# A fused attention and feed-forward kernel: the side work of an attention turn, and how many blocks of weighted sums go into the same turn

## The chip, the core and the metric

The kernel runs on one core of a Trainium2 chip. The metric is device time in microseconds (us) of one execution. The engines that matter are PE (TensorE matmuls), PEld (its weight loads), ACT (ScalarE, which computes the exponentials), DVE (VectorE), POOL (GpSimd) and the DMA queues.

## What is computed

Four sequences of 1024 tokens with 256 features go through attention with 16 heads of 16 features, and then through a gated feed-forward net with ternary weights. Layer norms surround both, and all of it is float32.

```python
qkv = layernorm(x) @ Wqkv.T                              # (4, 1024, 3*256)
scores = einsum('bhqd,bhkd->bhqk', q, k) / sqrt(16)      # 16 heads, 1024 x 1024 each
e = exp(clip(scores - max, -50, 50))
attn = e / (e.sum(-1) + 1e-6)
x = x + layernorm((attn @ v) @ Wout.T)
h = silu(ln(x) @ w1 * s1) * (ln(x) @ w2 * s2)            # 256 -> 1024
h = gelu(h @ h1 * s3); h = gelu(h @ h2 * s4)             # 1024 -> 1024, twice
x = x + layernorm(h @ w3 * s5)                           # 1024 -> 256
```

## The kernel before

The attention takes the first half of the time and is written as one long loop over **tiles** (L444). A tile is one sequence b, one group g of four heads, one half h of the queries (512 of them), one run c of 128 keys and one pair u of heads. There are 4 x 4 x 2 x 8 x 2 = 512 tiles. `exponentials(k)` (L450) makes one tile: two matmuls of 64 rows give the scores `s` in one of three PSUM buffers of two banks (L172), and one ACT instruction writes their exponentials `e` into a ring of eight tiles (RING, L27). `weigh(k)` (L460) takes two tiles, which are the four heads of one run of keys, and adds one **block** of weighted sums to `acc`: four products, which the profile counts as eight matmuls. Eight blocks make a **unit** (b, g, h). `rise(k)` (L467) lets DVE keep a running maximum `top` of those exponentials.

One pass of the loop at L874 is a **turn**. It makes three tiles (TURN, L28), weighs the blocks of all tiles that were made before this turn, and ends with `side.take()` (L569). With three tiles a turn and two a block, turns with one block and turns with two blocks alternate. A turn in which a unit ends stops at the end of the unit.

`Side` holds chains of steps. `take` runs down the chains and runs every step that is due: its gap, counted in turns since the step before it in its chain, has passed. Of the steps marked `tensor`, which use PE, it runs at most one in a turn. These tensor steps are:

- the projections of queries and keys (`project`, L325, 16 matmuls `p` in the profile), of values (`values`, L315, `pv`) and of the attention's output (`ending.project`, L517, `py`);
- four transposes of 128x128 (`pt` L310, `po` L512, `fpt` L692);
- the division of a finished unit (L476: eight transposes `po`, L484 and L486), which also borrows one of the three score buffers, so that the next turn makes its third tile only after its blocks (`side.borrowed`);
- sums of squares (`bound`, L360, `pn`) and one final gauge (`flag`, L378, `pr`), which together check that the exponentials can't overflow. For them ACT squares the rounded queries and keys (`squares`, L340).

All of them but the division write to the one bank of `ps_misc` (L174), from which DVE copies the result.

The steps of the next sequence are made by `prologue(b + 1)` while the present one is computed: norms and transposes to `xT`, the projections `qk[0]` of the first eight heads, from the end of group 1 on the values `v` and, five turns later, the projections `qk[1]` of the other eight heads, and then the checks. At the end of a unit `stack` (L425) sends the DMAs that lay out queries and keys for the group after the next, and `slots` (L431) lets POOL copy its values. Asserts hold that what they read has been projected by then. Chains of `check_weights` (L237) round the feed-forward weights in the same turns, on POOL and DVE.

After the last turn the feed-forward net runs (L809), for eight halves of sequences in turn. It is not touched by the change.

Of the kernel before, what the change touches and what calls it, by code (L numbers as in the profile page):

```python
# [70 lines left out]
class Step:  # L71


    def __init__(self, run, gap=0, tensor=True):
        self.run, self.gap, self.tensor = run, gap, tensor
# [39 lines left out]
def tile_fast(ctx: ExitStack, tc: tile.TileContext, x, wqk, wv, wo, w1, w1s, w2, w2s, h1, h1s, h2, h2s, w3, w3s, out, bad):  # L115
# [61 lines left out]
    with ExitStack() as actx, ExitStack() as rctx:  # L177
# [98 lines left out]
        def prologue(b, space, copy):  # L276
# [6 lines left out]
            def gather(h, i):  # L283
                def run():
                    if h == i == 0:
                        st["xT"] = work.tile([P, DC, S], F32, tag="xT", name=f"xT_{b}", bufs=1)
                    st["mv", h] = norms.gather(rows(h)[i : i + 2], i, st.get(("mv", h)))

                return run
# [16 lines left out]
            def transposes(h, c):  # L306
                def run():
                    pt = space(f"pt_{b}_{h}_{c}")
                    for i in range(TPQ):
                        nc.tensor.transpose(pt[:, i * P : (i + 1) * P], st["xn"][:, i, c * P : (c + 1) * P], ident)  # L310
                    copy(st["xT"][:, c, h * NQ : (h + 1) * NQ], pt)

                return run
# [24 lines left out]
            kinds = [(w, m) for w in range(2) for m in range(DC)]  # L338

# [8 lines left out]
            def total(m):  # L348
                def run():
                    if m == 0:  # L350
                        st["norm"] = work.tile([P, NT], F32, tag="norm", name=f"norm_{b}", bufs=1)
                        st["sum"] = work.tile([P, DC], F32, tag="sum", name="sum", bufs=1)
                        st["sum2"] = work.tile([P, DC], BF16, tag="sum2", name="sum2", bufs=1)
# [6 lines left out]
            def bound(h):  # L360


                def run():
                    pn = space(f"pn_{b}_{h}")
                    for k, (w, m) in enumerate(kinds):
                        nc.tensor.matmul(pn[SLOT * k : SLOT * (k + 1), :], heads_bf, st["sq", w, m], start=True, stop=True)
                    nc.vector.tensor_reduce(st["norm"][:, TPQ * h : TPQ * (h + 1)], pn.rearrange("p (t n) -> p t n", n=P), AX.X, ALU.max)
# [10 lines left out]
            def flag():  # L378
# [7 lines left out]
                qs, ks = (pr[0:1, 0 : 2 * P].rearrange("p (i w n) -> p i w n", i=2, w=2)[:, :, w, :] for w in range(2))  # L386
                top = work.tile([1, P // 2], F32, tag="ktop", name="ktop", bufs=1)
                nc.vector.tensor_reduce(top, ks.rearrange("p i n -> p n i"), AX.X, ALU.max)
# [3 lines left out]
                nc.vector.tensor_mul(bounds, qs, top.unsqueeze(1).to_broadcast([1, 2, P // 2]))  # L392
# [10 lines left out]
            qk = [[[Step(project(w, m, h), 1) for w in (1, 0)] for h in range(NH)] for m in range(DC)]  # L403
            v = [Step(values(t), 1) for t in range(0, NT, 2)]
            flags = [Step(total(m), 1, False) for m in range(DC)]
            for h in range(NH):
                flags += [Step(squares(w, m, h), 1, False) for w, m in kinds] + [Step(bound(h), 1)]
            return norm, xt, qk, v, flags + [Step(gauge, 0, False), Step(flag, 1)]
# [92 lines left out]
        def ending(b, h, copy):  # L501
# [41 lines left out]
            def residual(i):  # L543
# [7 lines left out]
                [Step(transposes(c), 1) for c in range(DC)] + [Step(project(t), 1) for t in range(0, TPQ, 2)]  # L551
# [5 lines left out]
        class Side:  # L557


            def __init__(self):  # L560
                self.first, self.rest, self.slot = [], [], 0
                self.borrowed = False
# [5 lines left out]

            def take(self):  # L569
# [3 lines left out]
                free = True  # L573
                for chain in self.first + self.rest:
                    steps = chain[0]
                    while steps and self.slot - chain[1] >= steps[0].gap and (free or not steps[0].tensor):
                        step = steps.pop(0)
                        chain[1] = self.slot
                        step.run()
                        free = free and not step.tensor  # L580

# [5 lines left out]
        accs, tops, ends, later = {}, {}, {}, {}  # L587

        def begin(b):

            if b + 1 < B:
                norm, xt, qk, v, flags = prologue(b + 1, misc, to_vector)

                qk1 = sum(qk[1], [])
                qk1[0].gap = 3
                later["rest"] = v, qk1 + [Step(lambda: side.add(flags), 0, False)]

                later["chain"] = side.add([Step(lambda: None, 0 if b else 4, False)] + sum((norm[h] + xt[h] for h in range(NH)), []) + sum(qk[0], []))

        def unit_end(b, g, h):  # L600
# [6 lines left out]
            if g == NG - 1:  # L607
                unit[0].extend(ending(b, h, to_scalar if (b, h) == (B - 1, NH - 1) else to_vector))
# [9 lines left out]
            if at < B:  # L618
                if at > b:
                    assert not later["chain"][0]  # L620
                stack(at, n)
                slots(at, n)()
            if g == NG - 3 and b + 1 < B:
                v, qk1 = later["rest"]
                assert not later["chain"][0]
                later["chain"][0].extend(v)
                side.add([Step(lambda: None, 5, False)] + qk1)
# [233 lines left out]
        side.add(early + v[2:] + [Step(slots(0, 0), 0, False), Step(slots(0, 1), 0, False)] + sum(qk[1], []) + [Step(lambda: side.add(flags), 0, False)])  # L861
# [4 lines left out]
        def make(end):  # L866

            nonlocal made
            for k in range(made, min(end, len(tiles))):
                assert k - weighed < RING  # L870
# [3 lines left out]
        while weighed < len(tiles):  # L874
            n = made
            make(n + TURN - side.borrowed)
            if made == len(tiles):
                n = made
            for k in range(seen, n - 1, 2):
                rise(k)  # L880
                seen += 2
            while weighed + 2 <= n:
# [9 lines left out]
            make(n + TURN)  # L892
# [243 lines left out]
```

## Time and profile before

| | us |
|---|---|
| three runs | 1326.97, 1328.48, 1330.16; median 1328.48 |
| the profiled execution's own time | 1328.08 |
| its span, from the first to the last instruction | 1326.3 |
| granted TensorE clock, mean | 0.993 |
| PE busy over the span | 1264.8 |
| ACT busy | 697.0 |
| DVE busy | 723.2 |
| POOL busy | 120.5 |

The page lists the costliest groups of instructions with their line, operation, output and input, count, busy time, mean duration, the idle time of the engine just before them and what ended it. These rows are of ACT's exponentials, of the blocks, of the scores and of the gelus of the feed-forward net:

```
L458 ACT ACTIVATE e<-s 128x1024 f32<-128x1024 f32 x512 | 486.3, 1035 | 121.7 <-PE s L457 109.0
L465 PE MATMUL acc<-e,vaug 128*32 128x512 f32 x2048 | 255.1, 600 | 1.4 <-POOL vaug L435 1.4
L457 PE MATMUL s<-sq,sk 64*128 64x512 f32 x1024 | 194.0, 449 | 25.5 <-ACT e L458 22.6
L739 ACT ACTIVATE a<-ph,h_scale 128x512 f32<-128x512 f32 x128 | 81.1, 686 | 306.9 <-PE ph L703 306.9
```

Busy time is the union of a group's instructions: the four matmuls of a block stand side by side in four column strips of the array, so that 2048 matmuls of 600 ns fill 255.1 us. Attention's first score product starts at 27.64 us and its last blocks at 647.37 us; the turns are numbered here from the first pass of the loop, 171 in all. The timeline of an engine lists merged instructions in order: start, duration, line, operation, count, and in brackets how long the engine sat idle before and for whom.

### The profile page before, as it was taken

The numbers are of one execution on the slowest core, as the hardware profiler recorded it, in microseconds if no ns is written. First come the engines' busy times: TensorE is split into PE (matmuls) and PEld (weight loads), VectorE is DVE, ScalarE is ACT, GpSimd is POOL, SyncE is SP. The second block draws the span as 40 slices with busy tenths as digits, with TensorE's granted clock in tenths as the row PEclk, the third lists the DMA queues.
The fourth block names the chain that finished last, engine by engine and source line by source line (L and its number), as shares of the span: only waits on it lengthen the run. The fifth ranks groups of instructions, "written<-read, shape, count | busy, mean of one in ns | idle before, by whom it ended". The sixth has DMA issues, their size and how long they took to land.

```text
span 1326.3 us, 21103 instructions
## 1 busy us (share of the span) xinstructions
PE 1264.8 (95%) x8194; PEld 777.2 (59%) x8194; DVE 723.2 (55%) x1561; ACT 697.0 (53%) x847; POOL 120.5 (9%) x166
## 2 busy tenths in 40 slices
PE   7889999999999999889999999999999999999996
PEld 3333333333333333333478888888888888888885
DVE  3575669756696556646573543636436263362523
ACT  3687788877887787988641422414123141231410
POOL 5221112101121000000010000000000000000000
PEclk8999999999999999999999999999999999999998
DMA  4665444444444333334230000000000000000000
GB/s 127 156 184 128 102 97 116 118 112 121 105 110 110 68 64 65 59 63 166 81 112 0 1 16 1 17 0 6 11 0 17 0 17 0 0 17 0 17 0 20
DMA packets 38670, 79.76 MB, mean 60 GB/s; under 512 B 11296, under 2 KB 21152, under 8 KB 38560
## 3 DMA queue, kind: packets, MB, share of 16 engines
q1 hardware_dynamic: 30672, 53.66, 18.4%
q0 software_dynamic: 7360, 24.12, 5.6%
q8 instruction: 67, 1.10, 0.4%
q10 hardware_dynamic: 528, 0.52, 0.1%
q14 instruction: 43, 0.35, 0.1%
HBM read 28.98 MB, written 15.73 MB: 34 GB/s over the span
## 4 chain that ended last, share of the span: by engine, by line
PE 75%; DVE 12%; ACT 8%; issue 2%; DMA 1%; SPq 1%; ACTq 0%; POOL 0%; POOLq 0%; DVEq 0%
PE ph L703 35%; PE acc L465 12%; PE s L457 8%; ACT e L458 7%; PE pz L756 4%; PE p L268 4%; PE pg L703 4%; PE py L268 2%; DVE top L474 2%; PE pv L268 2%; DVE sg L719 2%; PE po L486 1%; DVE ha_lo L708 1%; DVE o L274 1%; DVE st L93 1%
## 5 line engine op out<-in xcount | busy, mean ns | idle before, releaser
L458 ACT ACTIVATE e<-s 128x1024 f32<-128x1024 f32 x512 | 486.3, 1035 | 121.7 <-PE s L457 109.0
L465 PE MATMUL acc<-e,vaug 128*32 128x512 f32 x2048 | 255.1, 600 | 1.4 <-POOL vaug L435 1.4
L739 ACT ACTIVATE a<-ph,h_scale 128x512 f32<-128x512 f32 x128 | 81.1, 686 | 306.9 <-PE ph L703 306.9
L457 PE MATMUL s<-sq,sk 64*128 64x512 f32 x1024 | 194.0, 449 | 25.5 <-ACT e L458 22.6
L703 PE MATMUL ph<-hb_lo,h 128*128 128x512 f32 x512 | 199.4, 389 | 0.0
L703 PE MATMUL ph<-hb_hi,h 128*128 128x512 f32 x512 | 199.4, 389 | 0.0
L457 PEld LDWEIGHTS s<-sq,sk 64*128 64x128 f32 x1024 | 86.6, 184 | 164.7 <-ACT e L458 126.9
L474 DVE TENSOR_TENSOR top<-top,e 128x512 f32<-128x512 f32 x192 | 133.6, 696 | 35.7 <-ACT e L458 30.2
L740 DVE CAST ha_hi<-a 128x512 fp32r<-128x512 f32 x64 | 27.1, 423 | 157.9 <-ACT a L739 157.9
L465 PEld LDWEIGHTS acc<-e,vaug 128*32 128x32 f32 x2048 | 49.2, 108 | 106.1 <-issue 97.3
L103 POOL TENSOR_TENSOR rstd<-ve,minus_half 128x4 f32<-128x4 f32 (+1 forms) x33 | 37.5, 1137 | 791.1 <-DVE ve L101 791.1
L703 PEld LDWEIGHTS ph<-hb_lo,h 128*128 128x128 f32 x512 | 96.1, 188 | 20.1
L703 PEld LDWEIGHTS ph<-hb_hi,h 128*128 128x128 f32 x512 | 96.1, 188 | 20.2
L703 PE MATMUL ph<-ha_hi,sq 128*128 128x512 f32 x256 | 101.9, 398 | 0.4
L703 PE MATMUL ph<-ha_lo,sq 128*128 128x512 f32 x256 | 99.9, 390 | 0.0
L703 PE MATMUL ph<-ha_lo,sk 128*128 128x512 f32 x256 | 99.8, 390 | 0.0
L703 PE MATMUL ph<-ha_hi,sk 128*128 128x512 f32 x256 | 99.7, 390 | 0.0
L719 DVE SCALAR_TENSOR_TENSOR sg<-pg,w_scale,sg 128x512 f32<-128x512 f32 x64 | 47.1, 745 | 48.4 <-ACT sg L717 48.4
L717 ACT ACTIVATE sg<-pg,w_scale 128x512 f32<-128x512 f32 x64 | 43.4, 689 | 57.2 <-DVE ha_lo L708 48.4
L740 DVE CAST hb_hi<-a 128x512 fp32r<-128x512 f32 x64 | 27.0, 422 | 82.3 <-ACT a L739 82.3
L268 PE MATMUL p<-xT,wqk_sb 128*32 128x512 f32 x512 | 62.3, 608 | 0.9 <-ACT xT L271 0.9
L703 PEld LDWEIGHTS ph<-ha_hi,sq 128*128 128x128 f32 x256 | 48.2, 188 | 12.7 <-DVE sg L719 3.4
(145 smaller groups left out, 1642.9 us busy)
## 6 DMA issues: line engine op xcount, KB each, us to landing
w<-in_h_dram POOLq DMA_DIRECT2D x16, 512.0 KB, 4.5
h_r<-wr POOLq DMA_DIRECT2D x16, 512.0 KB, 3.8
sk<-ck1hi SPq DMA_DIRECT2D x64, 64.0 KB, 2.3
sk<-ck1lo SPq DMA_DIRECT2D x64, 64.0 KB, 2.3
sq<-cq1hi SPq DMA_DIRECT2D x64, 64.0 KB, 2.3
sq<-cq1lo SPq DMA_DIRECT2D x64, 64.0 KB, 2.3
h<-h_r SPq DMA_DIRECT2D x8, 512.0 KB, 7.1
sk<-ck0hi SPq DMA_DIRECT2D x56, 64.0 KB, 2.3
```

Of the source, the lines that this page charges most:

```text
L103: nc.gpsimd.tensor_tensor(rstd[:, :n], ve[:, :n], self.minus_half[:, :n], ALU.pow)
L268: nc.tensor.matmul(o[j : j + SLOT, :], w[:, j : j + SLOT], i, **flags)
L457: nc.tensor.matmul(s[:, a, :], stacks[1, g % 2, u][r, c * P : (c + 1) * P], stacks[0, g % 2, u][r, h * NQ : (h + 1) * NQ], start=True, sto ...
L458: nc.scalar.activation(pair(k)[:, u], s, AF.Exp)
L465: nc.tensor.matmul(acc[SLOT * i : SLOT * (i + 1), :], vaug[g % 2][:, c, i, :], pair(k)[:, i // 2, i % 2, :], start=c == 0, stop=c == NT - 1)
L474: nc.vector.tensor_max(top, top if c > 1 else pair(k - 2)[:, :, :, 0:P], pair(k)[:, :, :, 0:P])
L703: nc.tensor.matmul(p, homes[n][c][:, m * P : (m + 1) * P], half[:, c, :], start=c == 0 and k == 0, stop=c == len(homes[n]) - 1 and k == 1)
L717: nc.scalar.activation(sg, p[:, 0, :], AF.Silu, scale=scales["w1"][:, m : m + 1])
L719: nc.vector.scalar_tensor_tensor(sg, p[:, 1, :], scales["w2"][:, m : m + 1], sg, ALU.mult, ALU.mult)
L739: nc.scalar.activation(a, p[:, j, :], AF.Gelu, scale=scales[n][:, m : m + 1])
L740: nc.vector.tensor_copy(o[0][:, m, :], a)
L756: nc.tensor.matmul(p[t], half[:, c, t * P : (t + 1) * P], homes["w3"][c], start=c == 0 and k == 0, stop=c == HC - 1 and k == 1)
```

## The change

Four things are edited.

**1. A turn's blocks.** Steps get a mark `heavy`: all projections of queries, keys and output, and those of values for b > 0. Before it weighs, the loop asks `side.next_is_heavy()` whether the tensor step that this turn will run is heavy. If so, if two blocks or more are ready, if the ring has room for one tile more in the next turn, and if the next block is not the last but one of its unit, the turn weighs one block only, and the other is left to the turn after it.

**2. Heavy steps not in a row.** A heavy step is also `patient`: it is not due in a turn after one that ran a heavy step (`tired`). Exempt are the steps of `ending`, whose second projection gets a gap of two turns, and `qk[1]` of the sequences after the first, whose steps get a gap of two.

**3. Order of the side work.** The chain of the next sequence makes both halves' statistics first, and puts the normalisation of the second half between the projections of the first. Its first transpose waits until the sequence before has its `qk[1]` and `v` (`ready`), and `xT` is allocated there. `qk[1]` and `v` are appended to the same chain, and `slots` for a next sequence stands in that chain behind `v`.

**4. Sums by eight heads.** `bound(h)` with its four matmuls in one step becomes `bound(m, h)` with two, for m = 0 after `qk[0]` and for m = 1 after `qk[1]`: four steps instead of two for a sequence, each with a DVE maximum over 64 partitions instead of 128. `flag` reads the sums in the new order.

```diff
 class Step:
-    def __init__(self, run, gap=0, tensor=True):
-        self.run, self.gap, self.tensor = run, gap, tensor
+    def __init__(self, run, gap=0, tensor=True, heavy=False):
+        self.run, self.gap, self.tensor, self.heavy = run, gap, tensor, heavy
+        self.ready, self.patient = lambda: True, heavy
...
-            def bound(h):
+            def bound(m, h):
                 def run():
-                    pn = space(f"pn_{b}_{h}")
-                    for k, (w, m) in enumerate(kinds):
-                        nc.tensor.matmul(pn[SLOT * k : SLOT * (k + 1), :], heads_bf, st["sq", w, m], start=True, stop=True)
-                    nc.vector.tensor_reduce(st["norm"][:, TPQ * h : TPQ * (h + 1)], pn.rearrange("p (t n) -> p t n", n=P), AX.X, ALU.max)
+                    pn = space(f"pn_{b}_{m}_{h}")
+                    for w in range(2):
+                        nc.tensor.matmul(pn[SLOT * (2 * m + w) : SLOT * (2 * m + w + 1), :], heads_bf, st["sq", w, m], start=True, stop=True)
+                    own = slice(2 * SLOT * m, 2 * SLOT * (m + 1))
+                    nc.vector.tensor_reduce(st["norm"][own, TPQ * h : TPQ * (h + 1)], pn[own, :].rearrange("p (t n) -> p t n", n=P), AX.X, ALU.max)
...
-            qk = [[[Step(project(w, m, h), 1) for w in (1, 0)] for h in range(NH)] for m in range(DC)]
-            v = [Step(values(t), 1) for t in range(0, NT, 2)]
-            flags = [Step(total(m), 1, False) for m in range(DC)]
-            for h in range(NH):
-                flags += [Step(squares(w, m, h), 1, False) for w, m in kinds] + [Step(bound(h), 1)]
-            return norm, xt, qk, v, flags + [Step(gauge, 0, False), Step(flag, 1)]
+            qk = [[[Step(project(w, m, h), 1, heavy=True) for w in (1, 0)] for h in range(NH)] for m in range(DC)]
+            v = [Step(values(t), 1, heavy=b > 0) for t in range(0, NT, 2)]
+            flags = []
+            for m in range(DC):
+                flags.append([Step(total(m), 1, False)])
+                for h in range(NH):
+                    flags[m] += [Step(squares(w, m, h), 1, False) for w in range(2)] + [Step(bound(m, h), 1)]
+            flags[-1] += [Step(gauge, 0, False), Step(flag, 1)]
+            return norm, xt, qk, v, flags
...
-                [Step(transposes(c), 1) for c in range(DC)] + [Step(project(t), 1) for t in range(0, TPQ, 2)]
+                [Step(transposes(c), 1) for c in range(DC)] + [Step(project(t), 2 if t else 1, heavy=True) for t in range(0, TPQ, 2)]
...
+            def due(self, chain, slot, free):
+                step = chain[0][0] if chain[0] else None
+                if not step or slot - chain[1] < step.gap or step.tensor and not free:
+                    return None
+                return step if step.ready() and not (step.patient and self.tired) else None
+
+            def next_is_heavy(self):
+                for steps, at in self.first + self.rest:
+                    steps = list(steps)
+                    while step := self.due((steps, at), self.slot + 1, True):
+                        if step.tensor:
+                            return step.heavy
+                        at = self.slot + 1
+                        steps.pop(0)
+                return False
...
-                free = True
+                free, heavy = True, False
                 for chain in self.first + self.rest:
-                    steps = chain[0]
-                    while steps and self.slot - chain[1] >= steps[0].gap and (free or not steps[0].tensor):
-                        step = steps.pop(0)
+                    while step := self.due(chain, self.slot, free):
+                        chain[0].pop(0)
                         chain[1] = self.slot
                         step.run()
                         free = free and not step.tensor
+                        heavy = heavy or step.heavy
+                self.tired = heavy
...
+                steps = norm[0] + norm[1] + xt[0]
+                for i, step in enumerate(qk[0][0]):
+                    steps += [step, xt[1][i]]
+                steps += xt[1][TPQ // 2 :] + qk[0][1]
+
+                xt[0][TPQ // 2].ready = lambda: later["qk1"] == later["v"] == b
+                v = v + [Step(lambda: later.update(v=b + 1), 0, False)]
                 qk1 = sum(qk[1], [])
-                qk1[0].gap = 3
-                later["rest"] = v, qk1 + [Step(lambda: side.add(flags), 0, False)]
-
-                later["chain"] = side.add([Step(lambda: None, 0 if b else 4, False)] + sum((norm[h] + xt[h] for h in range(NH)), []) + sum(qk[0], []))
+                for step in qk1:
+                    step.gap, step.patient = 2, False
+                qk1 = qk1 + [Step(second_made, 0, False)]
+                later["rest"] = [Step(lambda: side.add([Step(lambda: None, 5, False)] + qk1), 0, False)] + v
+
+                later["chain"] = side.add([Step(lambda: None, 0 if b else 4, False)] + steps + [Step(first_made, 0, False)])
...
         while weighed < len(tiles):
-            n = made
-            make(n + TURN - side.borrowed)
+            n = end = made
+            end += TURN
+            make(end - side.borrowed)
             if made == len(tiles):
                 n = made
             for k in range(seen, n - 1, 2):
                 rise(k)
                 seen += 2
+
+            if n - weighed >= 4 and made - weighed + TURN - 2 <= RING and tiles[weighed][3] != NT - 2 and side.next_is_heavy():
+                n = weighed + 2
             while weighed + 2 <= n:
...
-            make(n + TURN)
+            make(end)
             if weighed < len(tiles):
                 side.take()
```

`first_made` and `second_made` add the checks of their eight heads as chains and note that the projections are there.

## The prediction

> **What bounds the kernel now.** I first read the busy times by stretch. The columns are the stretch, its length, then busy time and count of PE, PEld, DVE, ACT and POOL, then clock and DMA.
>
> ```profile
> 27.00:646.70 619.70, 579.41 (x4804) 217.87 (x4804) 391.55 (x837) 498.54 (x543) 87.48 (x119) 1.00 0.46 105
> 646.70:1326.30 679.60, 664.78 (x3274) 551.40 (x3270) 320.34 (x687) 191.03 (x292) 19.50 (x18) 0.99 0.05 16
> ```
>
> Only the first stretch, attention, is touched. There PE is busy 93% and ACT 80%. Then the waits of ACT and of PE in the turns (42 to 647 us), in total, times and longest:
>
> ```profile
> ACT e L458 <- PE s L457: 103.7, 110, 2.5
> ...
> ACT e L458 <- DVE top L474: 4.4, 6, 0.8
> ```
>
> ```profile
> PE s L457 <- ACT e L458: 22.6, 62, 0.7
> PE po L484 <- DVE top L474: 6.3, 9, 2.2
> ```
>
> Each of the two waits for the other: some turns are PE's, others ACT's. PE's timeline shows which. First four turns with a projection of the next sequence in each:
>
> ```profile
> 258.26 0.98 PE L457 MATMUL s<-sq,sk 64*128 64x512 f32 x6
> 259.17 1.07 PE L465 MATMUL acc<-e,vaug 128*32 128x512 f32 x8
> 260.05 1.90 PE L268 MATMUL p<-xT,wqk_sb 128*32 128x512 f32 x16
> 261.88 0.96 PE L457 MATMUL s<-sq,sk 64*128 64x512 f32 x6
> 262.77 1.92 PE L465 MATMUL acc<-e,vaug 128*32 128x512 f32 x16
> 264.51 1.90 PE L268 MATMUL p<-xT,wqk_sb 128*32 128x512 f32 x16
> 266.35 0.96 PE L457 MATMUL s<-sq,sk 64*128 64x512 f32 x6
> ```
>
> No bracket, so PE never waits: a turn with a projection and one block takes 261.88 - 258.26 = 3.62 us, with two blocks 266.35 - 261.88 = 4.47. Then turns without a tensor step:
>
> ```profile
> 572.51 0.97 PE L457 MATMUL s<-sq,sk 64*128 64x512 f32 x6
> 573.40 1.07 PE L465 MATMUL acc<-e,vaug 128*32 128x512 f32 x8
> 574.81 0.51 PE L457 MATMUL s<-sq,sk 64*128 64x512 f32 x2 [0.34 <-ACT e L458]
> 575.73 0.50 PE L457 MATMUL s<-sq,sk 64*128 64x512 f32 x2 [0.41 <-ACT e L458]
> 576.64 0.49 PE L457 MATMUL s<-sq,sk 64*128 64x512 f32 x2 [0.42 <-ACT e L458]
> 577.07 1.92 PE L465 MATMUL acc<-e,vaug 128*32 128x512 f32 x16
> 578.92 1.14 PE L457 MATMUL s<-sq,sk 64*128 64x512 f32 x6
> ```
>
> Here PE trickles its scores behind ACT. ACT's own timeline shows its pace and its squares:
>
> ```profile
> 291.30 5.61 ACT L458 ACTIVATE e<-s 128x1024 f32<-128x1024 f32 x6 [1.62 <-PE s L457]
> ...
> 324.55 0.65 ACT L344 ACTIVATE sq<-cq0hi 128x512 bf16<-128x512 f32 x1
> 325.07 2.88 ACT L458 ACTIVATE e<-s 128x1024 f32<-128x1024 f32 x3
> ```
>
> Six exponentials span 5.61, the first 1.03, so one follows another after 0.92 and three need 2.75. A square puts off what follows by 325.07 - 324.55 = 0.52. The pair of turns at 572.51 takes 6.41; two other such pairs (559.45 to 565.25, 623.77 to 629.60) take 5.80 and 5.83; mean 3.0 a turn.
>
> So a turn lasts **the longer of PE's content and about 3.0 us** (2.75 plus handing over), since three score buffers hold one turn's tiles and a long turn saves nothing for the next. PE's content, by pitches without a wait: 1.89 with one block (290.70 to 292.59), 2.75 with two (226.99 to 229.74), 0.86 for one more. A projection adds 1.72 (3.61 - 1.89), and 0.33 more right behind a division (253.46 to 258.26 took 4.80 against 4.47: the scores are split). A division adds 1.47 (250.10 to 253.46 took 3.36), four transposes 0.59, a sum 0.33 (`pn` 142.97 to 143.30), the gauge 0.57.
>
> **The sum before.** I applied the rules of the loop turn by turn, 171 turns in both kernels, for the turns 4 to 170. Before, they run from 41.97 to 646.70: 604.7 us. Counts by blocks in the turn:
>
> | turn holds | before 1 / 2 / 3 | after 1 / 2 / 3 |
> |---|---|---|
> | a projection | 24 / 29 / 0 | 48 / 4 / 1 |
> | a division | 21 / 10 / 0 | 18 / 13 / 0 |
> | another tensor step | 17 / 23 / 0 | 12 / 33 / 3 |
> | none | 22 / 21 / 0 | 11 / 23 / 1 |
>
> Before: projections 24 x 3.61 + 29 x 4.47 + 9 behind a division x 0.33 = 219.2. Divisions 21 x 3.36 + 10 x 4.22 = 112.8. Other steps 17 at the floor of 3.0 and 23 of 3.3 on average (17 transposes 3.34, four sums 3.08, two gauges 3.32) = 126.7. None: 43 x 3.0 = 129.0. Squares fall on turns at the floor and add 10.2 of their 32 x 0.52. Sum 597.9, 1.1% under the 604.7; the rest is about PE's waits for DVE.
>
> **A rule of the Trainium skill** (Perfetto Trace Analysis, Identifying the Most-Contended Engine) says that matmul occupancy is a poor measure of headroom, and that the share of time in LDWEIGHTS and the FLOPs done against the peak are better ones. That share is 217.87 / 619.70 = 35%, by which turns with projections would have room to shrink: if all 53 fell to the floor, 219.2 - 159 = 60 us would go. The four turns at 258.26, which have no gap, speak against it, and no term here rests on the rule.
>
> **Edits 1 and 2.** For example after the end of the second sequence's third unit the turns become: projection and one block, sum and two blocks, projection and one, gauge and two. The rule defers a block in 27 turns. Projections then cost 48 x 3.61 + 4 x 4.47 + 5.33 + 12 x 0.33 = 200.5, **18.7 less**. The blocks land elsewhere: divisions 18 x 3.36 + 13 x 4.22 = 115.3, **2.5 more**. Turns without a tensor step go from 43 to 35 and one block more fits under the floor at no cost: 34 x 3.0 + 3.61 = 105.6, **23.4 less**. That is cover, and where it is gone a block costs 0.86. All 512 tiles still need 171 turns.
>
> **Edits 3 and 4.** Eight sums more (0.33 of content each, and a floor that had hidden nothing else) and the blocks put beside small steps: 48 turns instead of 40, 12 x 3.0, 33 of about 3.25, 3 of 3.9 = 155.1, **28.4 more**. The moved checks put 13 of the 32 squares into turns with a projection, where ACT idles (3.27 against 3.61): squares add 3.8, **6.4 less**. DVE gets eight maxima of 0.69 (the `norm` rows now: 0.684 over 128 partitions; over 64 no row shows it, between 0.34 and 0.69; I take 0.69) and three tiny operations a sequence; it is busy 63%, behind them in its queue are maxima that nobody waits for until a unit ends. `slots` on POOL waits behind `v`: POOL idles for most of the stage and the copy (0.62) is due ten turns later. `stack` is issued at the same unit ends with the same 32 DMAs (267.11 to 290.61 at the end of this unit: 23.5 us, against 11 turns until it is read). The `ready` wait holds only side steps; the asserts' deadlines are met with the last `qk[1]` two turns ahead or more.
>
> The sum: -18.7 + 2.5 - 23.4 + 28.4 - 6.4 = **-17.6**. With a floor of 2.75 instead of 3.0 it is -14.3, with 3.2 (the pair at 572.51) -18.7. From the profiled execution's 1328.08 (span 1326.3): 1310.5. The runs' median, 1328.48, lies 0.4 above that execution, so 1311.
>
> The skill's same page (Optimizing Tensor Performance, Matmuls) says that independent matmul groups should rotate through PSUM banks. The side steps keep to one bank: the trace shows one wait for it, 1.24 us at 226.41. If each of the 29 steps right behind a projection (41 before) paid that, 36 us would come on; the rows at 260.05 and 264.51 start without any.
>
> **The rivals.**
> - *The deferred block makes the ring too short.* It is then full with eight tiles. The eighth exponential overwrites the tile weighed last, and must wait for DVE's maximum of it; ACT runs in order, so the next scores starve. For: `top` has held ACT up (0.8 at most, seen at 573.74). Against: that maximum is queued a turn earlier. At 0.82 x 27 = 22 the gain is gone and the time is 1328.1 - 17.6 + 22 = 1333. It decides from 17.6 / 27 = 0.65 a deferral.
> - *No change.* The turns are PE's already; what ACT no longer loses comes back as PE's waits for `top`, `o` and copies behind fuller turns. All 53 turns with a projection would have to lose 17.6 / 53 = 0.33. 1328.
> - *Half of it.* The same waits at 0.17 us a turn: 9 of 17.6 are lost, 1319.5.
> - *More.* In the first three sequences (turns 4 to 129) the floor no longer binds, because a short turn next to a long one makes it up: their turns would cost content alone, 13 us under the sum above (32 of them lie under the floor there, by 0.4 on average). PE's waits for DVE, the 604.7 - 597.9 = 7 us, go too. 1310.5 - 20 = 1291; halfway 1301.
>
> **Chances.** The forecast (1304 to 1317: terms 14 to 19, waits of 5 either way) 0.52; half (1317 to 1325.5) 0.17; more (1291 to 1304) 0.13; no change 0.07; slower 0.11. 0.2% of 1328.5, 2.7 us, is about what a measurement of this kernel can tell from no change. Faster 0.82, same 0.07, slower 0.11. The range leaves out the slower case, no change and the outer parts of half and more: 1299 to 1324.
>
> **What would show it.** Attention's last block near 630 instead of 650; ACT's wait for `s` from 103.7 to about 85, none over 2.5; 29 pairs of blocks beside a projection become 4 or 5; PE's wait for ACT under 18; squares beside projections. ACT waiting on `top` or `acc` over 0.65 in the deferred turns would prove the first rival, PE waiting on DVE the second. The feed-forward stretch should keep its 679.6; if that moves, the reasoning misses something.

## The result: no change, where 17.6 us were forecast

The changed kernel takes 1329.24 us (median of 20 runs, 1326.47 to 1331.82), the kernel before 1329.79 beside it (20 runs). The ratio is 0.9998, 95% interval 0.9991 to 1.0006. The profiled execution took 1327.01 us with a span of 1324.8. The forecast of 1311.0 and the range, 1299 to 1324, are missed.

The stretches of the changed kernel, up to its last block and behind it (columns as in the same view of before):

```profile
27.00:646.61 619.61, 580.49 (x4809) 217.62 (x4808) 398.66 (x850) 498.73 (x543) 85.95 (x117) 0.99 0.46 105
646.61:1324.80 678.19, 664.39 (x3268) 551.38 (x3266) 319.98 (x687) 190.75 (x292) 19.17 (x18) 0.99 0.05 16
```

The last block was expected near 630 and is at 646.61; before, the same three blocks start at 647.37. Feed-forward is nearly as it was (678.9 us from the start of the last blocks before, 678.2 now). The rows of the waits (total, times, longest), 42 to 647 us, of ACT and then of PE:

```profile
ACT e L462 <- PE s L461: 102.6, 109, 3.6
ACT e L462 <- DVE top L478: 6.0, 8, 0.8
```

```profile
PE s L461 <- ACT e L462: 11.4, 32, 0.7
PE po L488 <- DVE top L478: 9.7, 8, 2.2
PE po L490 <- DVE o L275: 3.9, 17, 0.2
PE py L269 <- DVE oT L275: 2.7, 2, 2.0
PE pt L311 <- DVE bounds L393: 1.9, 1, 1.9
PE pt L311 <- DVE cq1lo L335: 1.6, 1, 1.6
...
PE py L269 <- DVE norm L367: 1.2, 1, 1.2
...
PE pv L269 <- DVE norm L367: 1.1, 2, 0.6
PE p L269 <- DVE xT L275: 1.1, 1, 1.1
```

PE's wait for ACT fell from 22.6 to 11.4, under the 18 that was named, and turns with a projection hold one, two and three blocks 48, 4 and 1 times, as in the prediction's table: the rule works. ACT's wait for scores stayed (103.7 to 102.6), and its longest grew from 2.5 to 3.6. PE's waits for DVE grew, and those for `bounds`, `cq1lo` and `norm` are new among them. PE's timeline behind the end of the second sequence's third unit, the turns that the prediction wrote out:

```profile
263.07 1.93 PE L469 MATMUL acc<-e,vaug 128*32 128x512 f32 x16
264.83 0.39 PE L365 MATMUL pn<-sq,heads_bf 128*32 128x512 bf16 x2
...
266.12 1.06 PE L469 MATMUL acc<-e,vaug 128*32 128x512 f32 x8
267.00 1.90 PE L269 MATMUL p<-xT,wqk_sb 128*32 128x512 f32 x16
268.83 0.96 PE L461 MATMUL s<-sq,sk 64*128 64x512 f32 x6
269.72 1.92 PE L469 MATMUL acc<-e,vaug 128*32 128x512 f32 x16
```

Two blocks stand beside the sum (3.05 us from block to block) and one beside the projection (3.60 to the next block at 269.72, with 3.61 in the price list). Here the change does what was forecast.

**A ledger, turn by turn.** I took the start of the first block of every turn from PE's timeline, so that a turn lasts to the next one's first block, and set turns 4 to 170 against the prediction's price list, now turn by turn (PE's content, or a floor of 3.0 with 0.52 for each square). Counted from block to block the turns before take 603.3 us; the prediction's 604.7 was counted from score to score. The last three columns split what lies over the list: turns in which PE waited 0.5 us or more for DVE (without the waits for `o`, which the price of a division holds), turns of three blocks, all others.

| kernel | turns 4 to 170 | by the list | over it | with waits for DVE (turns) | three blocks (turns) | others |
|---|---|---|---|---|---|---|
| before | 603.3 | 597.2 | 6.1 | 4.7 (6) | 0 | 1.4 |
| changed | 603.4 | 579.5 | 23.9 | 17.6 (14) | 4.5 (5) | 1.8 |

The list's gain, 17.7, is in the trace: 148 turns of the changed kernel differ from their prices by 1.8 us in sum (single turns by up to 1.0 either way, which cancels). It was given back in 19 turns: 17.6 - 4.7 = 12.9 us to waits for DVE and 4.5 to the turns of three blocks. The 14 turns are of three kinds: six divisions that wait for the last maximum `top` (5.5 us over their prices), three projections that wait for a copy that they read (`oT`, `xT`; 5.9, with 1.6 of it from the clock, see the end), and five side steps that wait until DVE has read the one bank of `ps_misc` (`cq1lo`, `norm` three times, `bounds`; 6.1). Of the last kind there was one before, 0.3 over.

**The largest one** is where the second sequence starts. PE, then DVE, of the changed kernel:

```profile
205.37 1.07 PE L469 MATMUL acc<-e,vaug 128*32 128x512 f32 x8
208.42 2.80 PE L269 MATMUL py<-wo_sb,oT 128*32 128x256 f32 x32 [1.98 <-DVE oT L275]
211.15 1.65 PE L461 MATMUL s<-sq,sk 64*128 64x512 f32 x6
```

```profile
203.15 0.69 DVE L275 TENSOR_SCALAR oT<-po 128x512 f32<-128x512 f32 x1
203.75 0.68 DVE L258 SCALAR_TENSOR_TENSOR w<-w,wr 128x512 f32<-128x512 f32 x1
...
205.63 1.48 DVE L478 TENSOR_TENSOR top<-top,e 128x512 f32<-128x512 f32 x2
207.03 0.73 DVE L112 TENSOR_SCALAR y<-y,mv,rstd 128x256 f32<-128x256 f32 x2
207.68 0.69 DVE L275 TENSOR_SCALAR oT<-po 128x512 f32<-128x512 f32 x1
```

DVE has no gap here. Between the two copies `oT` stand a compare of rounded weights, the statistics of two tiles of the next sequence, two maxima and two normalisations, in the order in which they were issued. The kernel before, PE and then DVE:

```profile
205.41 1.92 PE L465 MATMUL acc<-e,vaug 128*32 128x512 f32 x16
207.15 1.91 PE L268 MATMUL py<-wo_sb,oT 128*32 128x256 f32 x32
```

```profile
205.26 0.69 DVE L274 TENSOR_SCALAR oT<-po 128x512 f32<-128x512 f32 x1
```

There two blocks stand ahead of the projection, and it starts 1.2 us after the copy's end. In the changed kernel one block stands there, 0.86 less cover, and the copy ends 3.0 us behind the start of that block instead of 0.5: the later copy is the larger part. The deferral isn't the reason. Without it (e6 below) one block stands there too, and the wait is the same:

```profile
207.94 1.06 PE L469 MATMUL acc<-e,vaug 128*32 128x512 f32 x8
210.99 1.93 PE L269 MATMUL py<-wo_sb,oT 128*32 128x256 f32 x32 [1.98 <-DVE oT L275]
```

In both, the gap of two turns in `ending` (edit 2) puts the second output projection of the first sequence's first half of queries into turn 44, where the kernel before had the next division, and this division and the end steps behind it come one turn later. No run undoes that gap alone. Over 50 us it looks like this, before and then changed (busy time of PE, PEld, DVE, ACT and POOL, clock):

```profile
200.00:250.00 50.00, 46.77 (x380) 18.29 (x372) 43.06 (x113) 42.93 (x48) 13.23 (x15) 1.00 0.58 139
```

```profile
200.00:250.00 50.00, 44.43 (x360) 16.49 (x362) 44.19 (x107) 34.72 (x39) 11.35 (x14) 0.97 0.50 117
```

DVE is busy 86 and 88% there (64% over the whole stretch), and PE is busy 2.3 us less. But a queue need not be full to be late. At 272 us DVE itself stands idle for the gauge's `pr`, with the maxima that the next division needs queued behind it:

```profile
270.30 0.68 DVE L478 TENSOR_TENSOR top<-top,e 128x512 f32<-128x512 f32 x1
272.14 0.28 DVE L388 TENSOR_REDUCE ktop<-pr 1x64 f32<-1x128 f32 x1 [1.16 <-PE pr L384]
...
273.51 1.20 DVE L354 TENSOR_REDUCE sum<-ck0hi 128x1 f32<-128x1024 f32 x1
274.63 1.83 DVE L478 TENSOR_TENSOR top<-top,e 128x512 f32<-128x512 f32 x2
```

PE's division started 1.76 us late for it. In the order of before the gauge was made elsewhere, and the division of this unit waited 0.28. The division of the changed kernel, then that of the kernel before:

```profile
276.61 0.63 PE L488 MATMUL po<-ident,top 128*128 128x128 f32 x4 [1.76 <-DVE top L478]
```

```profile
273.05 0.63 PE L484 MATMUL po<-ident,top 128*128 128x128 f32 x4 [0.28 <-DVE top L474]
```

**A turn of three blocks** on PE. In the turn before, behind a division, one of five pending tiles' blocks was weighed and three tiles were made, so that six tiles are pending:

```profile
244.16 0.73 PE L461 MATMUL s<-sq,sk 64*128 64x512 f32 x4
244.82 2.78 PE L469 MATMUL acc<-e,vaug 128*32 128x512 f32 x24
247.53 0.50 PE L461 MATMUL s<-sq,sk 64*128 64x512 f32 x2
```

The ring holds eight. Two scores fit, and the third is issued only behind the three blocks. ACT has nothing to do for 1.50 us, then has four exponentials in a row (3.77 us), and the turn takes 4.82 us instead of the 3.94 in the list (1.89 + 2 x 0.86 + 0.33).

### The profile page after: what moved, and what is told of

It reads as the page before. It is cut to its first block, busy times and chain, and to the rows that moved or that the text cites. A ratio compares the mean times of both kernels' runs of the same rounds, so it can differ in the third digit from the quotient of the medians.

```text
span 1324.8 us, 21087 instructions
## 1 busy us (share of the span) xinstructions
PE 1263.9 (95%) x8194; PEld 776.6 (59%) x8194; DVE 729.9 (55%) x1573; ACT 697.5 (53%) x847; POOL 119.6 (9%) x166
## 4 chain that ended last, share of the span: by engine, by line
PE 78%; DVE 11%; ACT 5%; issue 2%; DMA 2%; SPq 1%; POOL 0%; ACTq 0%; POOLq 0%; DVEq 0%
PE ph L749 35%; PE acc L469 13%; PE s L461 9%; PE pg L749 5%; PE pz L802 4%; ACT e L462 4%; PE p L269 4%; PE py L269 2%; PE pv L269 2%; DVE top L478 2%; DVE sg L765 1%; PE po L490 1%; DVE st L94 1%; DVE o L275 1%; DVE ha_lo L754 1%
## 5 line engine op out<-in xcount | busy, mean ns | idle before, releaser
L461 PE MATMUL s<-sq,sk 64*128 64x512 f32 x1024 | 192.3, 450 | 13.9 <-ACT e L462 11.4
L749 PEld LDWEIGHTS ph<-ha_hi,sq 128*128 128x128 f32 x256 | 48.3, 189 | 12.8 <-DVE sg L765 3.4
```

Source lines behind the costliest of these rows:

```text
L461: nc.tensor.matmul(s[:, a, :], stacks[1, g % 2, u][r, c * P : (c + 1) * P], stacks[0, g % 2, u][r, h * NQ : (h + 1) * NQ], start=True, sto ...
L749: nc.tensor.matmul(p, homes[n][c][:, m * P : (m + 1) * P], half[:, c, :], start=c == 0 and k == 0, stop=c == len(homes[n]) - 1 and k == 1)
```

## The experiments

Theory D: the change frees what was forecast, and DVE's in-order queue (with the ring, in five turns) gives it back. Rival P: each turn's price was wrong by a little. Rival C: only the clock, which fell behind the long wait at 208 us. Each median is set against runs of the kernel before that were taken beside it (1329.61 us for e1 to e4, 1328.61 for e5 to e8, 1329.50 for e9 to e12, 1330.03 for e13 to e15).

| run | median | ratio, 95% interval | difference |
|---|---|---|---|
| e1_nocount | 1319.28 | 0.9926, 0.9912 to 0.9939 | -10.3 |
| e2_before_nocount | 1325.18 | 0.9967, 0.9955 to 0.9979 | -4.4 |
| e3_joined | 1322.03 | 0.9944, 0.9931 to 0.9958 | -7.6 |
| e4_act | 1322.28 | 0.9949, 0.9936 to 0.9963 | -7.3 |
| e5_hold | 1321.37 | 0.9947, 0.9931 to 0.9964 | -7.2 |
| e6_nodefer | 1336.07 | 1.0053, 1.0040 to 1.0067 | +7.5 |
| e7_best | 1319.96 | 0.9931, 0.9915 to 0.9947 | -8.7 |
| e8_before_best | 1329.46 | 1.0001, 0.9991 to 1.0012 | +0.9 |
| e9_four | 1323.76 | 0.9962, 0.9948 to 0.9976 | -5.7 |
| e10_four_hold | 1315.73 | 0.9899, 0.9885 to 0.9913 | -13.8 |
| e11_four_hold_joined | 1311.49 | 0.9870, 0.9855 to 0.9885 | -18.0 |
| e12_oldorder | 1327.12 | 0.9985, 0.9976 to 0.9993 | -2.4 |
| e13_before_hold | 1326.49 | 0.9973, 0.9963 to 0.9982 | -3.5 |
| e14_nodefer_relieved | 1320.76 | 0.9933, 0.9919 to 0.9947 | -9.3 |
| e15_deferral_only | 1316.34 | 0.9893, 0.9878 to 0.9908 | -13.7 |

The same ledger for their profiled executions, one of each kernel:

| run | turns 4 to 170 | by the list | over it | with waits for DVE (turns) | three blocks (turns) | others |
|---|---|---|---|---|---|---|
| e1_nocount | 596.1 | 579.5 | 16.6 | 8.9 (11) | 4.5 (5) | 3.2 |
| e2_before_nocount | 601.5 | 597.2 | 4.4 | 1.5 (3) | 0 | 2.8 |
| e3_joined | 601.6 | 581.2 | 20.4 | 13.4 (10) | 3.6 (4) | 3.4 |
| e4_act | 601.5 | 579.5 | 22.0 | 11.6 (9) | 4.5 (5) | 5.9 |
| e5_hold | 595.4 | 579.5 | 15.9 | 8.1 (11) | 4.5 (5) | 3.3 |
| e6_nodefer | 610.9 | 591.7 | 19.2 | 15.8 (15) | 0 | 3.4 |
| e7_best | 596.9 | 581.2 | 15.7 | 2.4 (4) | 3.6 (4) | 9.8 |
| e8_before_best | 606.5 | 597.2 | 9.4 | 1.3 (1) | 0 | 8.0 |
| e9_four | 600.5 | 579.3 | 21.2 | 17.1 (14) | 0 | 4.2 |
| e10_four_hold | 592.9 | 579.3 | 13.6 | 7.9 (11) | 0 | 5.7 |
| e11_four_hold_joined | 588.3 | 580.5 | 7.7 | 4.4 (8) | 0 | 3.4 |
| e12_oldorder | 605.8 | 584.4 | 21.4 | 12.8 (10) | 5.1 (5) | 3.4 |
| e13_before_hold | 602.9 | 597.2 | 5.7 | 1.9 (3) | 0 | 3.8 |
| e14_nodefer_relieved | 597.8 | 590.4 | 7.4 | 4.3 (8) | 0 | 3.0 |
| e15_deferral_only | 593.5 | 583.1 | 10.4 | 6.8 (8) | 0 | 3.6 |

A row of this table holds what the granted clock did in that one execution. Read in stretches of 4 us from 44 to 644 us, the clock falls below 0.96, to 0.57 at the lowest, for one or two stretches at a time, and (1 - clock) x 4 us gives some 1.7 us for each such fall (an estimate from these stretches). There is none in before, e5, e6, e11 and e14, one in the changed kernel, e1, e2, e7, e9, e10 and e13, two in e4, e8 and e15, three in e3 and e12. So e12's turns are 2.5 us longer than before's here, and its median is 2.4 us lower; the medians decide, and differences of 2 us between rows of the table mean little. Rival C has a share of this size: the 20 runs of the changed kernel have a mean clock of 0.9906, the runs of the kernel before beside e1 to e15 0.991 to 0.992, e11 0.9932, and 0.001 of 1325 us is 1.3 us (an estimate again).

### Is it VectorE? e1 and its control e2

In both kernels:

```diff
-                    nc.vector.scalar_tensor_tensor(w, w, 1.0, r.bitcast(F32), ALU.mult, ALU.not_equal, accum_out=misses[:, i : i + 1])
```

> The changed kernel without VectorE's counting of rounded weights: 44 compares of about 0.76 us in the attention stage, 33 us of VectorE, are left out, and the count of misses stays at zero. Theory D (VectorE's in-order queue is full where a sequence starts, and TensorE waits there for copies and maxima): 8 to 14 us under the kernel before, with most of it at the starts of the second and third sequence. Rival P (the content or the handing over of each turn was mis-sized evenly; VectorE is only beside it): 1 to 4 us under the kernel before. Rival C (only the clock's dip after one long idle stretch of TensorE, near 208 us): about 1.6 us.

> The control: the kernel before without the same 44 compares (33 us of VectorE left out, the count of misses stays at zero). Theory D: only 1 to 4 us under the kernel before, since there VectorE is full in fewer places, so that this pair differs by 5 us or more. Rival P: the same gain as in the changed kernel, within 2 us. Rival C: nothing.

The same 44 compares (0.69 us each, and 0.08 to read the count) are worth 10.3 us in the changed kernel and 4.4 before: D's size in the first, a little over its 1 to 4 in the control, and 5.9 apart, where P wanted the same in both and C at most 1.6. The waits for DVE fall from 17.6 to 8.9. Most of what came off is where D wanted it: 2.7 us in turns 44 to 55 and 3.7 in 84 to 97, where the second and third sequence start, and 2.6 in turns 4 to 20. The wait of 1.98 us at 208 us is 0.98 in e1. P and C are out as the main cause.

### Three reliefs one by one: e3, e4, e5

e3 puts `bound(h)` back with its four matmuls behind `qk[1]` (the minus lines of that part of the change). e4:

```diff
-                    copy(st["xT"][:, c, h * NQ : (h + 1) * NQ], pt)
+                    to_scalar(st["xT"][:, c, h * NQ : (h + 1) * NQ], pt)
...
-                last = ending(b, h, to_scalar if (b, h) == (B - 1, NH - 1) else to_vector)
+                last = ending(b, h, to_scalar)
```

e5 (`crowded` starts as True):

```diff
+            if b < B - 1 and (g, h) == (NG - 1, 0):
+                side.crowded = True
+            if (g, h) == (0, NH - 1):
+                side.crowded = False
...
-        side.add([s for k in blocks for s in check_weights(*k)])
+        checks = [s for k in blocks for s in check_weights(*k)]
+        for s in checks:
+            s.ready = lambda: not side.crowded
+        side.add(checks)
```

> The changed kernel with the sums by eight heads undone: one sum over sixteen heads for each half of a sequence, behind the second group of projections, as before; the turns' rule and the order of the side steps stay. It takes eight maxima of about 0.69 us (5.5 us of VectorE) and eight sums' 0.33 us (2.6 us of TensorE) away. Theory D: 3 to 5 us under the kernel before. Rival P: about 2.6 us under it, and no less wait of TensorE for VectorE. A third theory, that the extra sums are where the gain went: 10 us or more under it.

> The changed kernel with the copies of the transposes of the next sequence and of the end steps (transposed outputs and their projection) on ScalarE instead of VectorE: about 25 us move from one queue to the other, some 6 us at each start of a sequence. Theory D: 8 to 16 us under the kernel before, and the waits of TensorE for VectorE at the starts of sequences go. Rival P: between 0 and 3 us over it, because the copies then stand between exponentials. Should ScalarE's queue be as full as VectorE's there, the gain stays under 4 us and TensorE's wait for exponentials grows from 11 to over 20 us.

> The changed kernel with the same work, but VectorE's counting of rounded weights (44 compares, 0.69 us each and 0.08 to read the count) waits while a sequence starts (from the end of the last group's first unit to the end of the next sequence's second unit, and at the very start) and is done between. Nothing is left out; some 15 compares, about 11 us of VectorE, move out of three crowded stretches. Theory D (VectorE's queue is full just there): 6 to 11 us under the kernel before, nearly what leaving the compares out gave (10). Rival P2 (VectorE's total, not its place, decides): 0 to 2 us under it, since the total stays.

e5 is the sharpest: nothing leaves DVE, the compares only stand elsewhere, and 7.2 us of the 10.3 come back. So place decides most of it, not the total. The largest wait falls from 1.98 to 0.97:

```profile
206.24 1.93 PE L269 MATMUL py<-wo_sb,oT 128*32 128x256 f32 x32 [0.97 <-DVE oT L275]
```

e3 gave 7.6, more than D's 3 to 5 and P's 2.6 and less than the third theory's 10; its profiled execution was the slowest of its five (1324.19), with three falls of the clock, so the ledger shows less of it than the median. e4 fell short of D's 8: the waits for DVE fell by 6.0, but 4.1 came back under "others". Of this 1.4 is one turn at 277 us with a clock of 0.57; that the rest is from copies between exponentials is likely, not shown.

### What the deferral does, and all reliefs together: e6, e7 and control e8

e6:

```diff
-            if n - weighed >= 4 and made - weighed + TURN - 2 <= RING and tiles[weighed][3] != NT - 2 and side.next_is_heavy():
+            if n - weighed >= 4 and made - weighed + TURN - 2 <= RING and tiles[weighed][3] != NT - 2 and False:
```

e7 has the edits of e3, e4 and e5; e8 has those of e4 and e5 in the kernel before.

> The changed kernel without the deferral of a block to the turn behind a projection; that a projection is not issued in the turn behind another one, the order of the side steps and the sums by eight heads stay. Five turns of three blocks go, which took 0.9 us each more than forecast because they hold four exponentials. Theory D: the waits for VectorE stay, the deferral's gain goes: 3 to 12 us slower than the kernel before. Rival: the deferral itself is what fills VectorE's queue (its maxima come later in the turn): then this is as fast as the kernel before or faster by up to 5 us.

> The changed kernel with three reliefs of VectorE together: the compares held back from the starts of sequences, the copies of the transposes and of the end steps on ScalarE, and one sum over sixteen heads. Nothing is left out. Theory D: 12 to 18 us under the kernel before, as far as the forecast of 17.6, with the waits of TensorE for VectorE halved. Rival (the three take the same waits away, so that they do not add up): 8 to 11 us under it.

> The control: the kernel before with the same reliefs (compares held back, copies on ScalarE; its sums are over sixteen heads already). Theory D: 0 to 4 us under the kernel before, so that with the reliefs the changed kernel is 10 us or more ahead of its control. Rival (the reliefs help any order of turns): 8 us or more under the kernel before, and the change itself is worth less than 5.

Without the deferral the waits for DVE stay (15.8): they come from where the steps stand, not from the deferred blocks. e7 met its rival: the waits shrink to 2.4, but "others" grow to 9.8, and the control has 8.0 there as well (1.5 and 3.2 of these are turns behind a fall of the clock). The control is no faster than the kernel before (+0.9), while e13, which has its held compares without its copies on ScalarE, is 3.5 us faster. So in the kernel before the copies cost more than they save; the next runs leave them out, and e13 is the cleaner control.

### The turns of three blocks, and the remedies added up: e9, e10, e11

e9:

```diff
-            if n - weighed >= 4 and made - weighed + TURN - 2 <= RING and tiles[weighed][3] != NT - 2 and side.next_is_heavy():
+            if n - weighed == 4 and made - weighed + TURN - 2 <= RING and tiles[weighed][3] != NT - 2 and side.next_is_heavy():
```

e10 adds e5's edit, e11 also e3's.

> The changed kernel, which defers a block only where exactly four tiles are pending, not where five or six are: 23 deferrals instead of 27, and no turn of three blocks is left but the last. By the sum of turns this costs nothing (579.3 against 579.5 us). Theory (the turns of three blocks start with six tiles in a ring of eight, so their third score is issued only behind the three blocks, ScalarE idles 1.5 us, and each of five turns takes 0.9 longer than its content): 4 to 5 us under the kernel before, with the waits for VectorE left as they are. Rival (these turns only moved a wait): within 1.5 us of the kernel before.

> Both remedies: deferral only at exactly four pending tiles, and the compares held back from the starts of sequences. Nothing is left out. If the two losses are separate: 7.3 + 4.5 = 12 us under the kernel before, between 10 and 14. If they are the same wait: 7 to 8 us under it.

> The same two remedies and one sum over sixteen heads instead of two over eight. If the sums over eight heads cost by themselves (six maxima less, each 0.69 us of VectorE, and the one bank that the side steps share is passed on less often): 13 to 16 us under the kernel before. If what they cost is the same crowding that holding the compares back has relieved: 10 to 13 us under it.

They add up: -5.7, -13.8, -18.0; the first is somewhat more than expected, the last 2 us more than the 16 of its range. e11 is the fastest kernel of the study, and with 1311.49 us it stands where the changed one was forecast; that the two agree so closely is luck, since holding the compares back helps the kernel before too (e13). Its last block starts at 631.54. Its waits, 42 to 632 us:

```profile
ACT e L460 <- PE s L459: 88.2, 102, 2.1
...
PE s L459 <- ACT e L460: 10.6, 29, 0.7
```

The prediction had named 630, about 85 with none over 2.5, and under 18.

### Which edit, and the control: e12 to e15

e12:

```diff
-                steps = norm[0] + norm[1] + xt[0]
-                for i, step in enumerate(qk[0][0]):
-                    steps += [step, xt[1][i]]
-                steps += xt[1][TPQ // 2 :] + qk[0][1]
+                steps = sum((norm[h] + xt[h] for h in range(NH)), []) + sum(qk[0], [])
...
-        accs, tops, ends, later = {}, {}, {}, {"qk1": None}
+        accs, tops, ends, later = {}, {}, {}, {"qk1": None, "v": None}
```

e13 is the kernel before with the edit of e5 alone. e14 is e6 with the edits of e3 and e5. e15 is e11 with the following edit; the gaps of two turns in `ending` and `qk[1]` stay in it:

```diff
-        self.ready, self.patient = lambda: True, heavy
+        self.ready, self.patient = lambda: True, False
```

> The changed kernel with the side steps of the next sequence in the order of before: norm and transposes of the first half, then norm and transposes of the second, then the four projections in a row, instead of both norms first and projections alternating with the second half's steps; the turns' rule and the sums over eight heads stay. Theory D (moving both norms into the start of a sequence filled VectorE's queue there): 3 to 6 us under the kernel before, and the wait of 1.98 us for the copied transposed outputs near 208 us shrinks. Rival (the order matters only for spacing projections, the crowding is from the end steps): 2 us under to 6 us over the kernel before, because projections then follow one another more closely.

> A cleaner control: the kernel before with the compares held back from the starts of sequences, and nothing else. If holding them back is worth what it is only because the change has filled VectorE's queue there: 0 to 3 us under the kernel before. If it helps any order of turns: 6 to 8 us under it, as in the changed kernel (7.2), and the change itself is then worth correspondingly less.

> The changed kernel with the two reliefs (compares held back, one sum over sixteen heads) but without any deferral of a block: of the rule of the turns only the spacing of projections is left. The sum of turns gives 590.4 us instead of 580.5; with 8 us of waits as in the version with deferral: 4 to 6 us under the kernel before. If the deferral is worth nothing and the reliefs are the whole gain: 14 us or more under it.

> The same two reliefs and the deferral at exactly four pending tiles, but projections may follow one another in neighbouring turns (no spacing). The sum of turns gives 583.1 us; with 8 us of waits: 10 to 14 us under the kernel before. If the spacing decides (a deferred block only lands beside the next projection): 6 us or less under it.

e12 lies between its two theories, and the ledger says why: the old order takes 4.8 us of waits away (17.6 to 12.8) and costs 4.9 by the list, as projections come closer together. So the new order brought part of the waits, not most. D also wanted the wait near 208 us to shrink, and it didn't (1.99). What brought the rest isn't shown by one run: not the deferral (e6), in part the split sums (e3: 17.6 to 13.4), and the end steps that come one turn later were not put back in any run. e13 is 3.5 under before, between its two theories: half of what the same edit gives in the changed kernel. e14 missed its 4 to 6 (9.3), and why isn't known; e15 met its 10 to 14. Against e11 the deferral is worth about 9 us, the spacing of projections (e15) about 4. With compares held back on both sides the change, its deferral limited to four pending tiles and its sums joined, is 18.0 - 3.5 = 14.5 us ahead.

## Why the prediction was wrong, point by point

- **What bounds the kernel**, the price list and the count of turns held: 148 undisturbed turns in sum within 1.8 us, the list's gain 17.7. By this ledger edits 1 and 2 free what was forecast, and in e11, with edit 4 undone and the deferral limited to four pending tiles, most of it arrives in the measured time (14.5 us against e13).
- **The step that failed** is the term that was put at nothing: PE's new waits for DVE. The text on edits 3 and 4 dismissed them because DVE "is busy 63%, behind them in its queue are maxima that nobody waits for until a unit ends". 63% is a mean over 620 us; where a sequence starts it was 86% before the change, and a unit ends every 16 to 24 us. The same text had worked out that moved checks cover squares on ACT, but did not set out what else is in DVE's queue in the turns into which the norms, copies, sums and, by edit 2, the end steps were moved. In the profiled execution this cost 12.9 us, 1.6 of them from the clock behind the longest wait. The length that it guessed for the new maxima was right (0.69 us over 64 partitions).
- **"That is cover, and where it is gone a block costs 0.86"** was said of PE's floor alone. A block ahead of a projection was also part of the cover of the copy that the projection reads: at 205 us 0.86 of cover went, and the copy came about 2.5 later against the block.
- **The rule on PSUM banks** of the Trainium skill (Perfetto Trace Analysis, Optimizing Tensor Performance, Matmuls), which the prediction set aside with one row of 1.24 us and two starts without a wait, pointed the right way: with the sums split, five steps waited for the one bank, 6.1 us over their prices; with the sums joined (e3) three did, 3.0 over. That is far under the 36 worked out there, and neither end was what the trace shows. No run gave the side steps a second bank.
- **The ring.** The rival's mechanism, an exponential that waits for DVE's maximum, came over its 0.65 in one deferred turn (0.82 at 224 us), and that turn kept its price of 3.61; over all turns these waits went from 4.4 to 6.0 us. But "It is then full with eight tiles" did matter, in 5 of the 27 deferred turns, by a path that the prediction lacked: the third score isn't issued until the blocks are. The list priced these turns by PE's content, and they cost 0.9 more each in the mean (without them, e9 is 5.7 us faster).
- **The rival "no change"** named most of the right waits (`top` and copies; those for `o` fell from 4.9 to 3.9) and got 0.07. Its price was spread over 53 turns as 0.33 each, which no row showed; in the trace it is 19 turns at 0.3 to 3.7 us. Working it out at the turns where DVE has most to do might have shown it as likely.

## What to carry to other kernels

When steps are moved, write out for each engine with an in-order queue what stands ahead of the instruction that another engine will wait for, in the busiest 10 us and not over the stage: a mean share of 63% hid stretches without a gap. A step that moves by one turn meets another queue and another cover, so look at the slack of each copy against its reader before calling it hidden. Where deadlines are loose, like the compares here, move them out of the crowded stretch first: nothing was left out, and it was worth 7.2 us in the changed kernel and 3.5 in the one before.

## What the hardware showed

The clock fell behind the wait at 208 us in the changed kernel (PE, PEld, DVE, ACT, POOL, then clock):

```profile
208.00:212.00 4.00, 3.58 (x36) 1.92 (x38) 3.33 (x10) 0.37 (x2) 0.00 (x0) 0.67 0.61 186
212.00:216.00 4.00, 3.81 (x28) 1.33 (x26) 3.71 (x9) 2.84 (x3) 2.38 (x3) 0.91 0.00 0
```

The projection took 2.80 us instead of 1.91 and the scores 1.65 instead of 0.96, some 1.6 us on top of the wait of 1.98. The same wait of 1.98 to 1.99 stands in the profiled executions of e3 and e12 (clock down to 0.60 and 0.65 in a stretch of 4 us, projection 3.12 and 2.76) and of e6 and e9 (clock 1.00, projection 1.93). One of 2.23 near 57 us left the clock at 1.00 in the kernel before and took it to 0.76 in e4. One of 1.76 to 1.77 near 275 us left it at 1.00 in the changed kernel and took it to 0.57 in e4:

```profile
276.00:280.00 4.00, 3.39 (x26) 1.63 (x30) 3.15 (x8) 1.70 (x2) 0.45 (x1) 1.00 0.82 209
```

```profile
276.00:280.00 4.00, 4.00 (x22) 1.07 (x24) 2.82 (x9) 1.94 (x2) 0.37 (x1) 0.57 0.83 191
```

So a wait of about 2 us puts the clock at risk and doesn't always lower it. The Trainium skill (TensorE: Matmul & The Clock Gate, What's actually happening) says that the gate watches a free-running window of about 3.4 us; that the outcome differs for equal waits fits a free-running window; that 2 us can be enough isn't said there. What else contributes to the fall stays open.
